# A two-layer graph attention kernel: the destination sums of every superchunk in three pieces, and node merging one step behind

## Chip, cores and metric

The kernel runs on one NeuronCore of a Trainium2 chip. The metric is the device time of one execution in microseconds (us). Five engines work on it with queues of their own: TensorE (PE) for matmuls, VectorE (DVE), ScalarE (ACT), GpSimd (POOL), which issues the row gathers, and SyncE (SP), which issues the other DMAs. Each engine takes its instructions strictly in the order of the program; semaphores make one wait for another.

## The reference

Two graph attention layers over N = 6250 nodes with 256 features and E = 200,000 edges sorted by destination. Cut to what matters (`_gat` gets one self-loop per node whose edge feature is the mean of the node's incoming ones; H is 4 heads of 64 in layer 0 and 1 head of 256 in layer 1):

```python
h = jnp.maximum(_layernorm(x, axis=-1), 0.0)
te = relu(edge_attr @ We + be) * exp(h @ Wo + bo)[src][:, None]
hx = (h @ Wg).reshape(n, H, F)
al = leaky_relu((hx*a_s).sum(-1)[src] + (hx*a_d).sum(-1)[dst]
                + ((te @ Wge).reshape(-1, H, F)*a_e).sum(-1), 0.2)
m  = segment_max(al, dst)
al = exp(al - m[dst]);  al = al / segment_sum(al, dst)[dst]
out = segment_sum(hx[src] * al[:, :, None], dst) + b
```

Layer 0 ends with `relu(out + h)`, layer 1 takes that as its input, and the result is x plus both layers' outputs with their residuals.

## The kernel before

**Tiling.** The 200,000 edges are 1563 chunks of 128. 24 chunks (C = 24) make a superchunk; there are 66 (NS = 66) a layer: 64 of 24 chunks, then one of 14 and one of 13. One step of the main loop in `edges` handles one superchunk, so there are 132 steps, k = 0 to 131, 66 for each layer. In a step, `st` is the superchunk at work, `nx` the next, `pv` the one before and `pf` the one before that. Edges lie so that partition p holds c consecutive edges of the sorted list.

**A prologue** (the first 97 us) normalizes x, multiplies it with the layer's weights and stores a table T0 of node rows in DRAM. Woven into it, `indices` prepares index data on DVE from loads of SP (`sc0`, `bcol`, `drow`, `r4`, `src`, `dpv`); `self.before` is the cast of `dpv`, and `index_group` reads it when it makes `fpen` (L544). Later index groups are made in the loop, seven pieces a step (three of four steps of layer 0).

**What a step does,** with the lines of the profile before:

- `gather(nx)`, L817: POOL issues one indirect DMA a chunk; each brings 128 table rows into `G`. Three `G` buffers rotate, so the gather of step k+1 needs the sums of step k-2 to be done.
- `rphase1(nx)`, L901 and L906: y = edge features times weights on PE in two halves, each followed by a relu on ACT into `R`. There is one `y` buffer. `rphase2` (L915) and `adst` (L974) turn R and the destinations' terms into `zad` on PE; `edge_rows` (L988, L991) transposes it to edges on DVE.
- `logits(st)`, L1002 to L1017: the logits and a forward and a backward segmented max scan on DVE. `ends` (L1025) transposes the scans' ends on PE; `links` (L1035, L1037 on DVE, L1042 on PE) scans over the partitions' borders and transposes the result back; `maxima` (L1052 to L1079) needs it.
- `spread` (L930, L931; once for two steps), `parts` (L955 to L958 on DVE, the matmul L960 on PE) and `blocks` (L967) prepare `nx`.
- `onehots` (L945): the 128 x 128 selection matrices `S` of a superchunk, two buffers.
- `scale` (L1110): the gathered rows times the exponentials; `carried` (L1095 to L1100) adds the share that a node carries over from the superchunk before.
- `sums` (L1120): 24 matmuls `u += S[i]^T G[i]`, which add the edges by destination; the profile counts two passes for each. One PSUM buffer holds `u`. `evict` (L1125) copies it to `U` on ACT; `carry` (L1131, L1133) picks the row that is carried over.
- `finish` (`merge`, `nodes0`, `nodes1`: L1144 to L1237): the self-loop is merged in, the softmax is divided out, the layer's result made, on DVE with small ACT steps. In layer 0, `rows1` (L1215, L1217) and `rows2` (L385) multiply it with layer 1's weights, and `rows3` (`table_row` L389 and L1227, then an SP DMA, L1256) stores the row of table T1. In layer 1, rows1 and rows2 are empty, and rows3 is the store of the output.

**Order.** The program's order is written out by hand (a manual schedule), so the loop body is the queue of every engine. In the loop before, rphase1(nx) comes first, the sums of `pv` stand whole between `parts(nx)` and the transpose in `links(st)`, the one-hots of `st` and finish of `pf` follow on DVE, then maxima, scale, carried, edge_rows(nx). The first step and those with s of 63 and 64 do their sums at once, at the end of the step. `last` handles the last superchunk of a layer (s = 65). In layer 0 it also issues the early gathers of layer 1's first step, whose rows from the last two windows of T1 are zeros that `turned_onehots` and `added` fill in by matmul.

The order of the loop before, as its lines:

```python
self.spread(nx)
self.parts(nx)
if pv and "u" not in pv:
    self.sums(pv)
self.links(st)
...
self.blocks(nx)
if k != self.NS:
    self.onehots(st)
if pf:
    drain(self.finish(pf))
```

Of the kernel before, what the change touches and what calls it, by code (L numbers as in the profile page):

```python
# [22 lines left out]
F32 = mybir.dt.float32  # L23
# [8 lines left out]
P = 128  # L32
C = 24
# [45 lines left out]
class Kernel:  # L79
# [311 lines left out]
    def indices(self, wp):  # L391


        nc, cp, a = self.nc, self.cp, self.a
# [11 lines left out]
        dpv = wp.tile([P, NS], I32, name="dpv", bufs=1)  # L406
        nc.sync.dma_start(dpv, a["dpv"])
        yield
        self.before = cp.tile([P, NS], F32, name="before")
        V.tensor_copy(self.before, dpv)  # L410
        scf = wp.tile([P, 11, NS], F32, name="scf", bufs=1)
        V.tensor_copy(scf, sc0)
        V.memset(scf[:, 0, 0:1], 0.0)
# [72 lines left out]
            V.tensor_scalar(chk[:, 4, :self.direct], base[0:1, :self.direct], float(N - P), None, op0=OP.is_gt)  # L486
        V.memset(self.bad[:, 0:1], 0.0)
        V.tensor_reduce(self.bad[0:1, 0:1], chk.rearrange("p a b -> p (a b)"), axis=AX.X, op=OP.add)
        yield

    def index_tiles(self):
# [79 lines left out]
    def edges(self, ctx):  # L571
        nc = self.nc
        self.gp += [self.pool(f"gath{i}", 1, ctx) for i in range(1, 3)]
        self.sp = self.pool("onehot", 2, ctx)
        self.lp = self.pool("loads", 2, ctx)
        self.wp = self.pool("work", 2, ctx)
        self.np_ = self.pool("nodes", 2, ctx)
        self.xp = self.pool("index", 1, ctx)
        self.ps_y = self.pool("ps_y", 1, ctx, space=PSUM)
        self.ps_1 = self.pool("ps_1", 1, ctx, space=PSUM)  # L580
        self.ps_f = self.pool("ps_f", 1, ctx, space=PSUM)
        self.lf = self.ps_1.tile([P, 512], F32, name="lf")
# [23 lines left out]
        pv = pf = None  # L606
        ahead, rest = 1, None
        for k, st in enumerate(steps):
            nx = steps[k + 1] if k + 1 < len(steps) else None
            for q in steps[k + 1:k + 3]:  # L610
                if q["L"] is st["L"] and "tw" not in q:
                    self.nodes(q)
            self.load_lb(k + 2)
            left = self.groups[ahead][0] - 2 - k if ahead < len(self.groups) else 99
            if rest is None and left <= 2:
                gi = self.index_load(ahead, self.xp)
                rest = self.index_group(ahead, self.xp, gi)
            if st["s"] + 1 == self.NS:
                self.last(st, pv, nx)
                pv = None  # L620
                continue
            self.gather(nx)
            drain(self.rphase1(nx))
            self.load_ea(k + 2)
            drain(self.logits(st))
            self.ends(st)
# [5 lines that stand above are left out]
            self.load_fl(k + 1)  # L632
# [17 lines left out]
            drain(self.scale(st))  # L650
            self.carried(st)
            at_once = k == 0 or self.NS - 3 <= st["s"]
            if at_once:
                self.sums(st)
            if pf:
                self.rows3(pf)
            self.edge_rows(nx)
            if rest is not None:
                for _ in range(7):
                    next(rest, None)  # L660
                if left <= 0:
                    drain(rest)
                    ahead, rest = ahead + 1, None
            pf, pv = pv, st

            if at_once:
                if pf:
                    drain(self.finish(pf))
                    self.rows1(pf)
                    self.rows2(pf)  # L670
                    self.rows3(pf)
                pf = None
                self.evict(st)
                self.carry(st)
            if k == 0 and self.early:
                self.redirect()
        self.flag()

    def last(self, st, pv, nx):

# [2 lines left out]
        if early:  # L683
            self.gather(nx, 0, self.src1)
            v = self.gp[(nx["k"] + 1) % 3].tile([P, C * 270], F32, name="v", tag="G").bitcast(BF)
            nc.sync.dma_start(v[:, :early * P], self.srow.partition_broadcast(P))
        if pv and "U" not in pv:
            self.sums(pv)
            self.evict(pv)
            self.carry(pv)  # L690
        now, half = (C, C) if st["L"].l else (0, C // 2)
        self.onehots(st, 0, now)
        drain(self.logits(st))
        self.ends(st)
        self.onehots(st, now, half)
        self.links(st)
        self.load_fl(st["k"] + 1)
        self.onehots(st, half)
        y = self.rphase1(nx) if nx else iter(())
        next(y, None)  # L700
        next(y, None)
        if nx:
            nc.vector.tensor_scalar(self.src, self.src, 2.0, None, op0=OP.mult)
        drain(self.maxima(st))
        drain(y)
        self.load_ea(st["k"] + 2)
        drain(self.scale(st, 3))
        self.carried(st)
        self.sums(st)
# [3 lines left out]
        if pv:  # L713
            if early:
                w0 = self.turned_onehots(nx, v, 0)
            self.rows1(pv)
            self.rows2(pv)
            self.rows3(pv)
        drain(self.finish(st))
        if early:  # L720
            w1 = self.turned_onehots(nx, v, 1)
# [389 lines left out]
                                    .to_broadcast([P, c1 - c0, H, L.F]), op=OP.mult)  # L1111
            yield

    def sums(self, st):
        nc, L, c = self.nc, st["L"], st["C"]
        G, S = st["G"], st["S"]
        st["u"] = u = self.ps_1.tile([P, 512], F32, name="u")
        for j in range(c):
            i = (j + 1) % c
            nc.tensor.matmul(u[:, :L.W], S[:, i, :], G[:, i, 0:L.W], start=(j == 0), stop=(j == c - 1))  # L1120

    def evict(self, st):
        L = st["L"]
# [263 lines left out]
def drain(g):  # L1387
    for _ in g:
        pass
# [93 lines left out]
```

## Time and profile before

| what | us |
| --- | --- |
| median of 3 runs | 4138.07 (4133.18 to 4142.69) |
| the profiled execution, its time | 4140.48 |
| the profiled execution, span from first to last instruction | 4138.4 |
| first gather of the loop starts | 97.38 |
| first L1035 of layer 0, step 0 | 141.32 |
| L1035 of the last step of layer 0 | 2113.39 |
| last gather starts | 4083.89 |
| mean granted PE clock, as a share of full | 0.78 |

Times in the profile are us from the span's start. A line of the timeline or of the chain of waits gives a start and a duration; in a group, the number after `x` is a count, then come busy us, mean ns of one and the idle time of the engine before them with what ended it. "Issue" is time in which the engine waited for nothing that the profile shows. The groups that this change touches most, besides those shown further on:

```profile
L1120 PE MATMUL u<-G,S 128*128 128x270 f32 (+1 forms) x6252 | 1714.1, 442 | 34.9 <-DVE G L1110 34.9
L901 PE MATMUL y<-ea,webd 64*128 64x384 f32 (+1 forms) x1056 | 512.4, 615 | 457.4 <-ACT R L906 455.3
L1110 DVE TENSOR_TENSOR G<-G,kps 128x6144 f32<-128x6144 f32 (+2 forms) x140 | 853.3, 6100 | 0.0
L988 DVE STREAM_TRANSPOSE rt<-zad 128x768 f32<-128x768 f32 (+1 forms) x130 | 124.4, 957 | 11.6 <-PE zad L974 11.6
```

### The profile page before, as it was taken

What the parts mean: (1) busy time and instruction counts of PE and PEld (TensorE: products, weight loads), DVE (VectorE), ACT (ScalarE), POOL (GpSimd) and SP (SyncE); (2) the same over time, 40 slices, a digit from 0 to 9 for tenths busy, and PEclk for the clock granted to TensorE, in tenths of its full rate; (3) what the DMA queues carried; (4) which work ended last, traced back from release to release, by engine and by line L of the source; (5) the groups of instructions that cost most, each with busy time, mean ns of one, the idle gap of its engine ahead of it and who ended that gap; (6) DMA issues with size and microseconds to landing.
All of it is one profiled execution on the core that took longest, in us unless ns stands there. A gap on an engine that the chain in (4) does not pass through costs nothing.

```text
span 4138.4 us, 34955 instructions
## 1 busy us (share of the span) xinstructions
PE 2815.1 (68%) x10144; PEld 1863.5 (45%) x10144; DVE 2872.6 (69%) x6572; ACT 545.2 (13%) x1256; POOL 2988.4 (72%) x3158
## 2 busy tenths in 40 slices
PE   7577777777676776777676666656566666756665
PEld 5344444444454444544454444434344444434344
DVE  7587777777877778778766666666666666666665
ACT  5111111111111111111111010100101010010100
POOL 2777777777777777777647777777777777777773
PEclk9677877778787787777877777878777777777777
DMA  6545555555554555555435455445545554554552
GB/s 203 155 135 153 149 142 147 147 146 143 154 149 137 154 147 141 149 149 149 125 102 151 132 143 141 137 137 144 141 133 141 141 137 137 145 141 133 141 139 61
DMA packets 246794, 584.74 MB, mean 141 GB/s; under 512 B 63161, under 2 KB 103639, under 8 KB 246529
## 3 DMA queue, kind: packets, MB, share of 16 engines
q0 software_dynamic: 150144, 422.82, 38.7%
q1 hardware_dynamic: 96035, 158.96, 12.3%
q8 instruction: 81, 1.33, 0.1%
q14 instruction: 118, 0.97, 0.1%
q10 hardware_dynamic: 416, 0.67, 0.1%
HBM read 547.98 MB, written 34.34 MB: 141 GB/s over the span
## 4 chain that ended last, share of the span: by engine, by line
POOL 35%; PE 27%; DVE 19%; issue 14%; DMA 2%; ACT 2%; DVEq 0%; ACTq 0%; SPq 0%; POOLq 0%
POOL G L817 35%; PE u L1120 21%; DVE G L1110 9%; PE y L901 3%; DVE lb L930 1%; DMA G<-T,src 1%; PE fin L1131 1%; DVE rt L988 1%; ACT R L906 1%; PE fin L1215 1%; DVE G L1099 1%; ACT carry L1133 1%; DVE G L1079 0%; DVE t1row L389 0%; DVE crow L1095 0%
## 5 line engine op out<-in xcount | busy, mean ns | idle before, releaser
L817 POOL DMA_INDIRECT G<-T,src x3114 | 2970.0, 954 | 1092.2 <-issue 996.5
L1120 PE MATMUL u<-G,S 128*128 128x270 f32 (+1 forms) x6252 | 1714.1, 442 | 34.9 <-DVE G L1110 34.9
L1120 PEld LDWEIGHTS u<-G,S 128*128 128x128 f32 x6252 | 1370.1, 222 | 386.8 <-issue 41.1
L1110 DVE TENSOR_TENSOR G<-G,kps 128x6144 f32<-128x6144 f32 (+2 forms) x140 | 853.3, 6100 | 0.0
L901 PE MATMUL y<-ea,webd 64*128 64x384 f32 (+1 forms) x1056 | 512.4, 615 | 457.4 <-ACT R L906 455.3
L901 PEld LDWEIGHTS y<-ea,webd 64*128 64x128 f32 x1056 | 214.3, 224 | 677.8 <-ACT R L906 535.7
L945 DVE TENSOR_TENSOR S<-kps,loc 128x3072 f32<-128x3072 f32 (+2 forms) x133 | 436.4, 3281 | 0.0
L1025 PE MATMUL lf<-ident,fb 128*36 128x128 f32 (+1 forms) x132 | 54.0, 409 | 533.8 <-DVE fb L1017 306.3
L1025 PEld LDWEIGHTS lf<-ident,fb 128*36 128x36 f32 (+1 forms) x132 | 15.8, 119 | 651.6 <-DVE fb L1017 363.3
L906 ACT ACTIVATE R<-y,webd 128x768 f32<-128x768 f32 x260 | 231.9, 892 | 566.4 <-PE y L901 566.2
L1056 DVE SCALAR_TENSOR_TENSOR m<-fpen,lf,m 128x24 f32<-128x24 bf16 (+1 forms) x66 | 16.5, 250 | 378.9 <-PE lf L1042 378.6
L1002 DVE TENSOR_TENSOR G<-rt,G 128x96 f32<-128x96 f32 (+1 forms) x132 | 30.2, 229 | 262.8 <-DMA G<-T,src 256.7
L915 PE MATMUL zad<-R,wea 128*64 128x384 f32 (+1 forms) x1056 | 205.4, 510 | 0.3 <-DVE aq L967 0.3
L1059 DVE TENSOR_TENSOR mt<-fpen,lf 128x96 f32<-128x96 bf16 (+1 forms) x66 | 16.7, 253 | 253.8 <-PE lf L1042 253.8
L1125 ACT ACTIVATE U<-u 128x270 f32<-128x270 f32 (+1 forms) x132 | 51.8, 392 | 815.8 <-PE u L1120 815.8
L960 PE MATMUL zad<-a,Q 128*128 128x12 bf16 (+1 forms) x132 | 23.7, 179 | 169.3 <-DVE a L958 169.3
L1158 ACT ACTIVATE mw<-mw,mg 128x2 f32<-128x2 f32 x66 | 19.7, 298 | 885.7 <-DVE mg L1157 885.7
L988 DVE STREAM_TRANSPOSE rt<-zad 128x768 f32<-128x768 f32 (+1 forms) x130 | 124.4, 957 | 11.6 <-PE zad L974 11.6
L930 DVE TENSOR_TENSOR lb<-lb,kps 128x1536 bf16<-128x1536 bf16 (+1 forms) x68 | 113.0, 1662 | 12.8 <-DMA lb<-locrow 12.8
L915 PEld LDWEIGHTS zad<-R,wea 128*64 128x64 f32 x1056 | 66.2, 139 | 92.5 <-issue 58.8
L1131 PE MATMUL fin<-U,lsel 128*1 128x270 f32 (+1 forms) x260 | 79.1, 385 | 41.5 <-ACT U L1125 22.5
L1035 DVE TENSOR_TENSOR_SCAN cl<-fl,cl,lf 4x129 f32<-4x129 f32 (+1 forms) x130 | 60.7, 467 | 56.3 <-PE zad L960 52.9
(213 smaller groups left out, 2269.9 us busy)
## 6 DMA issues: line engine op xcount, KB each, us to landing
G<-T,src POOLq DMA_INDIRECT x3114, 2.8
ea<-in_ea_dram SPq DMA_DIRECT2D x64, 768.0 KB
lb<-locrow SPq DMA_DIRECT2D x64, 384.0 KB
T<-t1row SPq DMA_DIRECT2D x66, 260.0 KB
tw<-T SPq DMA_DIRECT2D x66, 258.0 KB
tw<-T SPq DMA_DIRECT2D x66, 134.0 KB
tw<-in_x_dram SPq DMA_DIRECT2D x66, 128.0 KB
out_dram<-fb SPq DMA_DIRECT2D x64, 128.0 KB
```

What stands on the lines that cost most here:

```text
L817: nc.gpsimd.indirect_dma_start(out=G[:, c, 0:L.TW], out_offset=None, in_=self.rows[L.l][0:n * (1 + L.l), :], in_offset=bass.IndirectOffset ...
L901: nc.tensor.matmul(y[:, o], self.webd[l][r, :], ea[r, w], start=True, stop=True)
L906: nc.scalar.activation(R[:, i, :32 * c].rearrange("p (b n) -> p b n", b=2), y.rearrange("p (b n) -> p b n", b=2)[:, :, :16 * c], AF.Relu, ...
L915: nc.tensor.matmul(st["zad"][i * PH:(i + 1) * PH, o], self.wea[l][0], R[:, i, w], start=True, stop=False)
L930: V.tensor_tensor(lb[:, :, :n], lb[:, :, :n], self.k_part.unsqueeze(2).to_broadcast([P, i, n]), op=OP.is_equal)
L945: nc.vector.tensor_tensor(st["S"][:, c0:c1, :], self.k_iota.unsqueeze(1).to_broadcast(w), self.loc[:, o + c0:o + c1].unsqueeze(2).to_broad ...
L988: V.transpose(rv[:, :32 * c].rearrange("p (b n) -> p b n", b=2), z.rearrange("p (b n) -> p b n", b=2)[:, :, :16 * c])
L1025: self.nc.tensor.transpose(self.lf[0:e.shape[1], 1:P + 1], e, self.ident)
L1035: V.tensor_tensor_scan(cl[:H, :], fl[:H, :], lf[:H, 0:P + 1], init, op0=OP.add, op1=OP.max)
L1110: nc.vector.tensor_tensor(v, v, pw[:, c0:c1, :].unsqueeze(3) .to_broadcast([P, c1 - c0, H, L.F]), op=OP.mult)
L1120: nc.tensor.matmul(u[:, :L.W], S[:, i, :], G[:, i, 0:L.W], start=(j == 0), stop=(j == c - 1))
L1131: nc.tensor.matmul(pr[0:1, :L.W], self.lsel[:, s:s + 1], U[:, :L.W], start=True, stop=True)
```

## The change

All steps but the first and the last of each layer take a new body, `tight`. The sums of a superchunk come in three pieces (`pieces` gives 12 and 16 for 24 chunks): chunks 0 to 11 at the end of its own step, 12 to 15 in the next step between `parts(nx)` and the transpose of `links`, 16 to 23 behind that transpose. The one-hots are made for `nx` at the end of the step, and `finish` works on `pv` (one step behind, not two), also at the end of the step. rphase1(nx) moves from the head of the step to behind rows2. `last` takes the same pieces through `meet`. In the prologue, the cast of `dpv` moves from the start of `indices` to its end.

```diff
@@ indices
-        self.before = cp.tile([P, NS], F32, name="before")
-        V.tensor_copy(self.before, dpv)
...
+        yield
+        self.before = cp.tile([P, NS], F32, name="before")
+        V.tensor_copy(self.before, dpv)
@@ edges, the loop
+        tight = 1
...
             if st["s"] + 1 == self.NS:
                 self.last(st, pv, nx)
-                pv = None
+                pv = pf = pr = None
+                continue
+            if st["s"] >= tight:
+                self.tight(st, pv, pr, nx)
+                self.index_on(left)
+                pr, pv = pv, st
                 continue
...
-            at_once = k == 0 or self.NS - 3 <= st["s"]
-            if at_once:
+            enter = st["s"] + 1 == tight
+            if enter:
+                self.sums(st, 0, self.pieces(st)[0])
...
+            if enter:
+                self.onehots(nx)
...
+    def pieces(self, st):
+        c = st["C"]
+        return (c + 1) // 2, c - c // 3
+
+    def meet(self, st, pv, nx):
+        p1, p2 = self.pieces(pv) if pv else (0, 0)
+        drain(self.logits(st))
+        self.ends(st)
+        if nx:
+            self.spread(nx)
+            self.parts(nx)
+        if pv:
+            self.sums(pv, p1, p2)
+        self.links(st)
+        if pv:
+            self.sums(pv, p2)
+        self.load_fl(st["k"] + 1)
+
+    def tight(self, st, pv, pr, nx):
+        final = nx["s"] + 1 == self.NS
+        self.gather(nx)
+        self.meet(st, pv, nx)
+        self.blocks(nx)
+        if final:
+            self.evict(pv)
+            self.carry(pv)
+            if pr:
+                self.rows1(pr)
+                self.rows2(pr)
+                self.rows3(pr)
+            drain(self.finish(pv))
+            drain(self.maxima(st))
+            self.rows1(pv)
+            self.rows2(pv)
+        else:
+            drain(self.maxima(st))
+            self.evict(pv)
+            self.carry(pv)
+            if pr:
+                self.rows1(pr)
+                self.rows2(pr)
+        drain(self.rphase1(nx))
+        self.load_ea(st["k"] + 2)
+        self.rphase2(nx)
+        self.adst(nx)
+        if final:
+            self.rows3(pv)
+        drain(self.scale(st))
+        self.carried(st)
+        self.sums(st, 0, self.pieces(st)[0])
+        if pr and not final:
+            self.rows3(pr)
+        self.edge_rows(nx)
+        self.onehots(nx)
+        if not final:
+            drain(self.finish(pv))
@@ last
-        if pv and "U" not in pv:
-            self.sums(pv)
-            self.evict(pv)
-            self.carry(pv)
...
-        self.onehots(st, half)
-        y = self.rphase1(nx) if nx else iter(())
-        next(y, None)
-        next(y, None)
+        if not pv:
+            self.onehots(st)
+        self.meet(st, pv, None)
...
         drain(self.maxima(st))
-        drain(y)
-        self.load_ea(st["k"] + 2)
+        if pv:
+            self.evict(pv)
+            self.carry(pv)
         drain(self.scale(st, 3))
...
             self.rows3(pv)
+        if nx:
+            drain(self.rphase1(nx))
+            self.load_ea(st["k"] + 2)
         drain(self.finish(st))
@@ sums
-    def sums(self, st):
+    def sums(self, st, a=0, b=C):
...
-        for j in range(c):
+        for j in range(a, min(b, c)):
             i = (j + 1) % c
-            nc.tensor.matmul(u[:, :L.W], S[:, i, :], G[:, i, 0:L.W], start=(j == 0), stop=(j == c - 1))
+            nc.tensor.matmul(st["u"][:, :L.W], S[:, i, :], G[:, i, 0:L.W], start=(j == 0), stop=(j == c - 1))
```

More of the change, by code (lines that the diff above doesn't have):

```diff
@@ L604, in edges @@
         self.edge_rows(steps[0])
-        pv = pf = None
-        ahead, rest = 1, None
+        pv = pf = pr = None
+        tight = 1
+        self.ahead, self.rest = 1, None
         for k, st in enumerate(steps):
@@ L613, in edges @@
             self.load_lb(k + 2)
[L614 to L617, printed above, removed]
+            left = self.groups[self.ahead][0] - 2 - k if self.ahead < len(self.groups) else 99
+            if self.rest is None and left <= 2:
+                gi = self.index_load(self.ahead, self.xp)
+                self.rest = self.index_group(self.ahead, self.xp, gi)
             if st["s"] + 1 == self.NS:
                 self.last(st, pv, nx)
-                pv = None
+                pv = pf = pr = None
+                continue
[3 more added lines that the diff above has]
+                pr, pv = pv, st
                 continue
@@ L651, in edges @@
             self.carried(st)
-            at_once = k == 0 or self.NS - 3 <= st["s"]
-            if at_once:
+            enter = st["s"] + 1 == tight
+            if enter:
+                self.sums(st, 0, self.pieces(st)[0])
+            elif st["s"] == 0:
                 self.sums(st)
@@ L657, in edges @@
             self.edge_rows(nx)
[L658 to L672, printed above, removed]
+            if enter:
+                self.onehots(nx)
+                if pv:
+                    drain(self.finish(pv))
+                pr = pv
+            elif st["s"] == 0:
                 self.evict(st)
                 self.carry(st)
+            self.index_on(left)
+            pf, pv = pv, st
             if k == 0 and self.early:
@@ L677, in edges, with index_on @@
         self.flag()
+    def index_on(self, left):
+        if self.rest is not None:
+            for _ in range(7):
+                next(self.rest, None)
+            if left <= 0:
+                drain(self.rest)
+                self.ahead, self.rest = self.ahead + 1, None
+    def pieces(self, st):
[51 more added lines that the diff above has]
+        if not final:
+            drain(self.finish(pv))
     def last(self, st, pv, nx):
@@ L686, in last @@
             nc.sync.dma_start(v[:, :early * P], self.srow.partition_broadcast(P))
-        if pv and "U" not in pv:
-            self.sums(pv)
-            self.evict(pv)
-            self.carry(pv)
[L691 to L697, printed above, removed]
-        self.onehots(st, half)
-        y = self.rphase1(nx) if nx else iter(())
-        next(y, None)
-        next(y, None)
+        if not pv:
+            self.onehots(st)
+        self.meet(st, pv, None)
         if nx:
@@ L704, in last @@
         drain(self.maxima(st))
-        drain(y)
-        self.load_ea(st["k"] + 2)
+        if pv:
+            self.evict(pv)
+            self.carry(pv)
         drain(self.scale(st, 3))
@@ L1112, in scale @@
             yield
-    def sums(self, st):
+    def sums(self, st, a=0, b=C):
         nc, L, c = self.nc, st["L"], st["C"]
         G, S = st["G"], st["S"]
-        st["u"] = u = self.ps_1.tile([P, 512], F32, name="u")
-        for j in range(c):
+        if a == 0:
+            st["u"] = self.ps_1.tile([P, 512], F32, name="u")
+        for j in range(a, min(b, c)):
             i = (j + 1) % c
-            nc.tensor.matmul(u[:, :L.W], S[:, i, :], G[:, i, 0:L.W], start=(j == 0), stop=(j == c - 1))
+            nc.tensor.matmul(st["u"][:, :L.W], S[:, i, :], G[:, i, 0:L.W], start=(j == 0), stop=(j == c - 1))
     def evict(self, st):
```

## The prediction

> **What bounds the kernel now.** I read the page first. No engine is full: GpSimd (POOL) leads with 72%, almost all of it row gathers, and the idle time in front of the gathers is "issue", time that waits for nothing.
>
> ```profile
> PE 2815.1 (68%) x10144; PEld 1863.5 (45%) x10144; DVE 2872.6 (69%) x6572; ACT 545.2 (13%) x1256; POOL 2988.4 (72%) x3158
> L817 POOL DMA_INDIRECT G<-T,src x3114 | 2970.0, 954 | 1092.2 <-issue 996.5
> ```
>
> Then I read the chain of waits by layer. In layer 1 it is gathers alone, each with its issue gap:
>
> ```profile
> 2999.75 0.95 POOL G L817
> 3000.70 0.30 issue
> ```
>
> One gather is issued every 1.25 us, so a step of 24 cannot be shorter than 30.04 us. In layer 0 the chain leaves POOL and runs PE, VectorE (DVE), PE. One step of it:
>
> ```profile
> 1018.05 0.17 PE zad L960
> 1018.22 12.45 PE u L1120 x48
> 1030.66 0.19 PE lf L1042
> ...
> 1033.66 6.40 DVE G L1110
> ...
> 1041.44 0.90 DVE rt L988
> ...
> 1048.00 0.01 PE zad L960
> ```
>
> The 24 sums (48 passes) stand between the matmul of parts (L960) and the transpose of links (L1042) that maxima waits for. The starts of L1035 give 30.35 us a step from step 2 to step 63 of layer 0 (194.75 to 2045.90, 61 steps), 0.3 over POOL's pace. The waits of that stretch show what is at stake:
>
> ```profile
> DVE mt L1059 <- PE lf L1042: 249.0, 61, 5.2
> POOL G L817 <- PE lf L1042: 22.9, 23, 5.4
> ```
>
> DVE waits 4.1 us a step for that transpose, but POOL loses only about 23 us in the whole layer. That is the most layer 0 can win, since past it the gathers bound; layer 1 can win nothing in steady state.
>
> **What hides what today.** While PE runs the sums, DVE runs the one-hots (3.26 us from start to next start) and finish (4.94 us, 1022.21 to 1027.15), then waits. PE in turn has the next step's y (L901) done early: two matmul pairs per step, one in this step's slack, one behind a long idle.
>
> ```profile
> 1018.95 3.35 DVE L945 TENSOR_TENSOR S<-kps,loc 128x3072 f32<-128x3072 f32 x1
> 1004.20 1.55 PE L901 MATMUL y<-ea,webd 64*128 64x384 f32 x4
> 1011.29 2.92 PE L901 MATMUL y<-ea,webd 64*128 64x384 f32 x4 [5.54 <-ACT R L906]
> ```
>
> **The new step in layer 0, from one L960 to the next.** Only 4 of 24 sums stay before the transpose, 8 follow it, and 12 move to the end of the step before. But PE's program order is now: 4 sums, transpose, 8 sums, lsel, rows1, rows2, y, y, rphase2, adst, first 12 sums of the step. DVE's edge_rows (L988 before) waits for adst, and behind it in DVE's queue stand onehots(nx), finish(pv), the index pieces and the next step's logits; for those PE waits (ends, parts), and POOL waits for the sums that free a buffer. So I add PE's chain up to adst, and the DVE work behind it:
>
> - 24 passes on the path. I took the 60 whole layer-0 groups of 48 passes row by row: the first 24 last 7.87 us (6.71 to 8.74), the last 24 5.47, since PE starts them at half clock after idling. In the new step PE idles before them as well (the first 12 sums end some 8 us before the next L960), so 7.87. Transpose 0.19.
> - From the end of the sums to the end of rows2, with rows of 1030.7 to 1033.2 and 1003.2: eviction with its gaps 0.48, lsel 0.63, carry with gaps 0.46, rows1 0.45, h1T with gaps 0.52, rows2 1.04: 3.58.
> - y 1.55, relu with gaps 1.05, y 1.55, relu 1.05 (layer 1 shows this pair, 3016.14 to 3021.24): 5.20.
> - rphase2: one of its four matmuls needs only the first half of R and runs under the second relu; three take 1.06 of 1.44; adst 0.50: 1.56.
>
> That is 18.40 us until edge_rows may start. DVE itself is there after 3.83 (8 passes) + 0.19 + 10.6 (L1042's end to L988: 1030.85 to 1041.44) = 14.65, so it stalls 3.75. Then edge_rows 1.44, one-hots 3.26, finish 4.94, logits 1.90 with 0.3 of semaphore gaps, spread 1.98 in every second step (0.99), parts and L960 0.92, index pieces (1.9, 0.9 and 0.45 in three of four steps) 0.8: 14.55. Together 32.95. The one-hots and finish, 8.20 us, were free under the sums; now they lie on the path, and for that 5.47 us of sums left it. Against 30.35: +2.6 us a step, 61 steps, +159 us.
>
> **The clock in that chain.** The prices above are at full clock. These two stretches of PE's windows show it drop:
>
> ```profile
> 1003.87:1007.28 3.41, 1.88 (x6) 0.67 (x4) 3.41 (x1) 0.00 (x0) 2.50 (x4) 1.00 0.39 107
> 1007.28:1010.70 3.42, 0.00 (x0) 0.00 (x0) 3.39 (x7) 0.46 (x2) 2.67 (x3) 0.50 0.44 120
> ```
>
> The columns are length, busy PE, PE loads, DVE, ACT, POOL, then the granted clock. A stretch of 3.41 us in which PE was busy 1.88 (55%) is followed by clock 0.50; one with 1.55 (46%, 3017.73 to 3021.14) too; one with 2.33 (68%, 1034.58 to 1038.00) keeps 1.00. Between the sums and the first 12 sums PE would be busy 0.63+0.45+1.04+3.10+1.56 = 6.8 of 10.3 us, 66%, just at that line. Ends of the term: nothing, if the clock holds; if it falls at once, 1.37 for each y (2.92 against 1.55), 1.0 and 0.3 for rphase2 and adst (2.83 and 0.82 at 142.47 and 145.23 against 1.51 and 0.50, three quarters of the first), and an estimate of 2.1 for lsel, rows1 and rows2 at double their rows: 6.1. I take 2.0: the second y, rphase2 and adst slow (2.7) in three steps of four, because the gaps (1.05 twice) lie there. 61 steps: +122 us.
>
> [...]
>
> **The rest.**
> - Prologue: the cast of dpv moves behind the checks. Now DVE stands 7.41 us for its DMA (33.7 to 41.1), and DVE is on the chain from there to 88 us. The next instruction reads sc0, queued first of that batch; its landing isn't seen, so 0 to -7.4. I take -6.5, as no other wait on a load stands in the rows after it. Nothing reads `before` until L544 at 96 us.
> - Steps 0 to 2: the one-hots and finish fall on the path while nothing of sums(0) was in step 1's way before (it ran at once, under step 0's end). With the rows at 154 to 194 step 2 starts 3 us later (0 to +5).
> - End of layer 0: sums(63) need not run whole behind scale(63) (2069.51, 14.22 us) and rows(63) move up. From L960 of step 63 to the first gather of layer 1 now: 2046.2 to 2113.6, 67.4. New: to adst 15.4 (14 chunks), edge_rows to the next L960 13.6, in step 64 7.87+3.58 to rows2(62), t1row 0.4, finish(63) 4.9, rows 2.1, y and relu 4.2, t1row's exp, store and landing 3: 55. The rest of the transition gives some back to the half clock: -10 (-4 to -14).
> - Tail: from logits(129) at 4052.95 to the end now 85.4. New: 22.1 for step 129 (2.8 to L960, 7.65, 0.19+0.48+0.60, y and relu 3.6, 1.1, edge_rows 0.9, one-hots 1.9, finish 2.95), 22.1 for step 130 (finish now ahead of maxima and waiting for all sums), and 19.7 for the last (logits to the first scaled piece 6.4, 26 passes 8.55, eviction, finish, store 4.8): 63.9. With half clock for the y's, -18 (-12 to -22).
> - Layer 1, steady: no rows, finish 2.95. The same sum is 7.65+0.19+1.1+5.2+1.56, edge_rows 1.2, 3.26, 2.95, logits 1.4, spread 0.99, parts 0.9: 26.4, and 4 more with a low clock; below 30.04. So 0, hidden by POOL.
> - SP: the ea load waits for the later y, with the t1row store behind it, but it has a step's time until it is read: 0. Moving index pieces and load_fl: 0.
>
> Sum on the profiled span: 4138.4 + 159 + 122 - 6.5 + 3 - 10 - 18 = 4388 us. The profiled execution took 4140.5 with its 2 us around the span, the median of the runs 4138.07, so the span stands for the median. I forecast **4385**.
>
> **Rivals.**
> - *The chain is on the path, the clock holds* (0.2): 4388 - 122 = 4266. For it: 66% is at the edge, the longest gap is 1.05. Against: two drops at 46 and 55%.
> - *The whole chain runs at half clock* (0.13): 6.1 x 61 = 372 in place of 122: 4638 at the end; with half of the excess, 4510. For it: once low, PE rose only after a full stretch (0.50 still at 2.88 of 3.41, 1017.52 to 1020.93).
> - *DVE does not stall and POOL bounds layer 0* (0.1): 61 steps at 30.04 save 19: 4138 - 19 - 6.5 - 13 - 21 = 4079, faster. It decides when the loop is under 30.04, 2.9 us less than my sum; if PE were warm, the 24 passes would take 5.47, 2.4 less. For it: DVE's wait of 4.1 goes. Against: PE idles before them in every step of the trace.
> - *It nets to nothing* (0.02): the warm loop at about 30.8 with the gains at both ends.
>
> The forecast has 0.55. **Range** 4210 to 4540: below lies the faster case and a part of the warm one, above the half-clock end. A change under 0.2% (8 us) is what a measurement of this kernel cannot tell from none. Faster 0.1, same 0.02, slower 0.88.
>
> **What would show it.** Layer 0's L1035 rows 33 to 36 us apart; DVE's L988 row (L1052 after) waiting for adst 3.5 us or more in each layer-0 step; the wait of L1059 down to about 2; y rows of 2 to 2.9 us; POOL waiting several us a step for sums in layer 0 and none in layer 1, whose steps stay at 30.04; a first gather near 91 us; some 15 us less from the last gather to the end. Wrong if edge_rows doesn't wait, or if layer-0 steps are at 30.

## The result, and the profile after

The changed kernel takes 4400.64 us (median of 4 runs, 4395.32 to 4404.33); the kernel before, on the same chip, 4140.38 us (4133.18 to 4143.16). The ratio is 1.064, with a 95% interval of 1.0621 to 1.0659: 6.4% slower. The forecast was 4385. The profiled execution took 4403.65 us, its span is 4401.8.

From the page, the busy line and three groups, the last beside its line in the kernel before (in a group: count, busy us, mean ns of one, and after the second bar the idle time before them with what ended it):

```profile
PE 3128.6 (71%) x10144; PEld 1901.9 (43%) x10144; DVE 2879.3 (65%) x6571; ACT 559.1 (13%) x1256; POOL 2973.3 (68%) x3158
L881 POOL DMA_INDIRECT G<-T,src x3114 | 2955.0, 949 | 1383.1 <-issue 966.0
L1052 DVE STREAM_TRANSPOSE rt<-zad 128x768 f32<-128x768 f32 (+1 forms) x130 | 127.1, 978 | 779.3 <-PE zad L1038 779.3
L979 PE MATMUL zad<-R,wea 128*64 128x384 f32 (+1 forms) x1056 | 434.6, 737 | 7.7 <-ACT R L970 7.4
L915 PE MATMUL zad<-R,wea 128*64 128x384 f32 (+1 forms) x1056 | 205.4, 510 | 0.3 <-DVE aq L967 0.3
```

The work is the same, the count of matmuls too, yet PE is busy 313 us longer (2815.1 before). Of these, some 229 us are rphase2's (L979, L915 before), whose recorded time now also takes in part of the second relu. The clock isn't lower on the whole (mean granted clock 0.799, 0.780 before); what changed is where in the step it is low. POOL's gathers stand idle 291 us longer (1092.2 before), and their issue gaps are no part of that. One DVE instruction, the first of edge_rows, has 779 us of waiting in front of it.

Where the 263.4 us of the span (4401.8 - 4138.4) are, from the starts of DVE's first links scan (L1035 before, L1099 after) and of the gathers:

| stretch | before | after | difference | predicted |
|---|---|---|---|---|
| to the first gather | 97.38 | 88.58 | -8.8 | -6.5 |
| from there to the scan of step 0 | 43.94 | 42.64 | -1.3 | not priced |
| steps 0 to 2 of layer 0 | 53.4 | 59.1 | +5.7 | +3 |
| steps 2 to 63 (61 steps) | 30.35 each | 35.11 each | +290.5 | +281 |
| step 63 to the first gather of step 67 | 107.6 | 103.6 | -4.0 | -10 |
| from there to the last gather | 1930.4 | 1925.8 | -4.6 | 0 |
| last gather to the end | 54.5 | 40.4 | -14.1 | -18 |

So the time is lost in the middle steps of layer 0. The list of waits of the changed kernel, 200 to 2050 us, DVE and POOL (who waited for what: us in total, times, longest):

```profile
DVE rt L1052 <- PE zad L1038: 352.7, 53, 10.0
DVE mt L1123 <- PE lf L1106: 154.7, 52, 3.1
...
POOL G L881 <- PE u L1185: 276.4, 52, 10.2
```

Before, the first was absent, the second (as L1059) was 4.1 us a step and the third 23 us in all. Now DVE stands 6.7 us a step for adst and POOL 5.3 us a step for the sums that free a gather buffer. PE's timeline of one such step, start and length:

```profile
1035.68 4.76 PE L1185 MATMUL u<-G,S 128*128 128x270 f32 x16
1040.93 0.62 PE L1196 MATMUL fin<-U,lsel 128*1 128x270 f32 x2 [0.49 <-ACT U L1190]
1042.02 0.44 PE L1280 MATMUL fin<-ident,fb 128*128 128x128 f32 x2 [0.48 <-ACT carry L1198]
1042.99 1.14 PE L385 MATMUL fin<-wg,h1T 128*128 128x260 f32 x4 [0.53 <-ACT h1T L1282]
1044.06 1.55 PE L965 MATMUL y<-ea,webd 64*128 64x384 f32 x4
1046.67 1.97 PE L965 MATMUL y<-ea,webd 64*128 64x384 f32 x4 [1.05 <-ACT R L970]
1048.56 3.27 PE L979 MATMUL zad<-R,wea 128*64 128x384 f32 x8
1051.77 0.50 PE L1038 MATMUL zad<-lb,aq 128*128 128x384 bf16 x2
```

And DVE's, which starts edge_rows when the last of these ends, then does the one-hots, then finish, and reaches the next logits at 1062.95:

```profile
1052.30 0.98 DVE L1052 STREAM_TRANSPOSE rt<-zad 128x768 f32<-128x768 f32 x1 [6.43 <-PE zad L1038]
...
1053.69 3.35 DVE L1009 TENSOR_TENSOR S<-kps,loc 128x3072 f32<-128x3072 f32 x1
...
1062.95 0.26 DVE L1066 TENSOR_TENSOR G<-rt,G 128x96 f32<-128x96 f32 x1
```

The second y takes 1.97 us where the first takes 1.55. The row of rphase2, 3.27 us, is not to be held against its 1.51 in the kernel before, since its first matmul now starts while the second relu still runs:

```profile
1048.67 0.90 ACT L970 ACTIVATE R<-y,webd 128x768 f32<-128x768 f32 x1 [2.06 <-PE y L965]
```

From the end of that relu to the end of rphase2 it is 2.27 us here. Over the 61 steps it is 1.56 in the 20 steps with the clock at 1.00 there, and 2.55 in the 41 with a mean of 0.50 to 0.74. Two windows of PE show the clock fall (length, busy PE, loads, DVE, ACT, POOL, granted clock):

```profile
1044.27:1047.68 3.41, 2.36 (x7) 1.13 (x7) 1.57 (x6) 0.90 (x1) 2.61 (x3) 1.00 0.40 102
1047.68:1051.09 3.41, 3.41 (x9) 1.16 (x8) 0.00 (x0) 0.99 (x2) 2.50 (x4) 0.50 0.47 121
```

PE was busy 69% of the first; the next has half the clock although PE is recorded as busy all through it.

### The profile page after: what moved, and what is told of

It reads as the page before. It is cut to its first block, busy times and chain, and to the rows that moved or that the text cites. A ratio compares the mean times of both kernels' runs of the same rounds, so it can differ in the third digit from the quotient of the medians.

```text
span 4401.8 us, 35044 instructions
## 1 busy us (share of the span) xinstructions
PE 3128.6 (71%) x10144; PEld 1901.9 (43%) x10144; DVE 2879.3 (65%) x6571; ACT 559.1 (13%) x1256; POOL 2973.3 (68%) x3158
## 4 chain that ended last, share of the span: by engine, by line
POOL 31%; PE 30%; DVE 17%; issue 13%; DMA 5%; ACT 4%; DVEq 0%; ACTq 0%; SPq 0%; POOLq 0%
POOL G L881 31%; PE u L1185 16%; PE y L965 5%; DMA G<-T,src 5%; PE zad L979 4%; DVE S L1009 3%; DVE lb L994 2%; ACT R L970 2%; PE fin L385 1%; DVE rt L1052 1%; PE fin L1196 1%; PE zad L1038 1%; DVE fb L1079 1%; DVE al L1070 1%; DVE al L1068 1%
## 5 line engine op out<-in xcount | busy, mean ns | idle before, releaser
L1185 PE MATMUL u<-G,S 128*128 128x270 f32 (+1 forms) x6252 | 1757.2, 440 | 16.0 <-DVE G L1174 16.0
L1185 PEld LDWEIGHTS u<-G,S 128*128 128x128 f32 x6252 | 1335.2, 219 | 294.3 <-DVE G L1174 17.9
L965 PE MATMUL y<-ea,webd 64*128 64x384 f32 (+1 forms) x1056 | 534.5, 638 | 141.1 <-ACT R L970 136.3
L979 PE MATMUL zad<-R,wea 128*64 128x384 f32 (+1 forms) x1056 | 434.6, 737 | 7.7 <-ACT R L970 7.4
L1009 DVE TENSOR_TENSOR S<-kps,loc 128x3072 f32<-128x3072 f32 x132 | 436.3, 3305 | 0.0
L979 PEld LDWEIGHTS zad<-R,wea 128*64 128x64 f32 x1056 | 140.6, 189 | 289.5 <-issue 174.9
L1139 ACT ACTIVATE kps<-mt 128x100 f32<-128x100 f32 (+1 forms) x132 | 29.8, 226 | 1419.1 <-DVE mt L1133 725.1
L1123 DVE TENSOR_TENSOR mt<-fpen,lf 128x96 f32<-128x96 bf16 (+1 forms) x66 | 16.6, 252 | 188.2 <-PE lf L1106 188.2
L385 PE MATMUL fin<-wg,h1T 128*128 128x260 f32 x264 | 88.1, 464 | 36.7 <-ACT h1T L1282 36.7
L1024 PEld LDWEIGHTS <-Q 128*128 128x128 bf16 x132 | 13.6, 103 | 215.4 <-DVE a L1022 198.5
```

The costliest lines, as they stand in the source:

```text
L385: self.nc.tensor.matmul(ps[:, :L.MW], hT[:, k, :], self.wg[L.l][:, k, :], start=(k == 0), stop=(k == 1))
L965: nc.tensor.matmul(y[:, o], self.webd[l][r, :], ea[r, w], start=True, stop=True)
L979: nc.tensor.matmul(st["zad"][i * PH:(i + 1) * PH, o], self.wea[l][0], R[:, i, w], start=True, stop=False)
L1009: nc.vector.tensor_tensor(st["S"][:, c0:c1, :], self.k_iota.unsqueeze(1).to_broadcast(w), self.loc[:, o + c0:o + c1].unsqueeze(2).to_broad ...
L1185: nc.tensor.matmul(st["u"][:, :L.W], S[:, i, :], G[:, i, 0:L.W], start=(j == 0), stop=(j == c - 1))
```

## The experiments

Each kernel ran beside the kernel before on the same chip, where that took 4138 to 4143 us (experiment 10 apart); ratios are to it. "A step" is the mean from step 2 to step 63 of layer 0.

**1. y back at the head of the step.**

```diff
 def tight
         self.gather(nx)
+        drain(self.rphase1(nx))
+        self.load_ea(st["k"] + 2)
         self.meet(st, pv, nx)
...
-        drain(self.rphase1(nx))
-        self.load_ea(st["k"] + 2)
         self.rphase2(nx)
```

> The changed kernel with one thing put back: in the middle steps the next step's rphase1 (both y matmuls and both relus) and its ea load stand at the head of the step again, ahead of logits, as before the change. Theory A (the loss is PE's chain sums, evict, rows, y, relu, y, relu, rphase2, adst, which keeps DVE from edge_rows with the one-hots and finish queued behind): without y the chain is 5.2 us shorter and more of it runs at full clock, the wait of the transpose in edge_rows (L1052) falls from 6.7 us to under 1.5 us a step, layer-0 steps fall from 35.1 to the gathers' pace, 30.0 to 30.6, and the time is 4085 to 4130 us, below the kernel before. Rival B (the loss is that the 8.2 us of one-hots and finish no longer lie beside the 24 sums, whatever stands before them): the steps stay above 33.5 us and the time above 4300. Rival C (splitting the sums in three costs it: PE cold at each piece): also above 4300, with the PE rows of the sums unchanged and the wait of L1123 still 3 us.

4078.91 us, ratio 0.985 (0.9834 to 0.9867), 6 us under the expected range; 30.01 us a step, as expected. Waits, 200 to 2050 us:

```profile
DVE mt L1123 <- PE lf L1106: 177.0, 61, 3.1
...
DVE rt L1052 <- PE zad L1038: 20.9, 24, 1.3
...
POOL G L881 <- issue: 440.8, 1447, 0.3
```

The wait for adst falls from 6.7 to 0.3 us a step, and POOL waits for nothing but its own issue. From the first sum behind parts to the end of adst it takes 14.2 us on average, 20.85 in the changed kernel. The pieces of the sums stand as they were, with their 2.9 us wait of L1123: neither they (rival C) nor the place of the one-hots and finish (rival B) costs anything that shows at the pace of the gathers, once y is out of the chain.

**2. One-hots and finish ahead of edge_rows.** y stays late.

```diff
-        self.edge_rows(nx)
         self.onehots(nx)
         if not final:
             drain(self.finish(pv))
+        self.edge_rows(nx)
```

> The changed kernel with one order turned on DVE: onehots of the next step and finish of the step before are issued ahead of edge_rows instead of behind it; PE's order stays. Theory A (DVE stands 6.7 us a step for adst with 8.2 us of work queued behind that needs none of it): the one-hots and finish fill the wait, the layer-0 step loses 5 us or more and is held by the gathers at 30.0 to 30.6 us, the time is 4085 to 4130 us. Rival B (PE's chain is the bound by itself, from one adst to the next, and DVE only waits on it): steps stay at 34 us or more, the time at 4350 or more. Rival D (the index pieces or the rows chain set the step): no change either.

4080.09 us, ratio 0.985 (0.9834 to 0.9866), 5 us under the expected range; 30.07 us a step. Waits of DVE and POOL:

```profile
DVE G L1066 <- DMA G<-T,src: 113.5, 54, 6.4
...
DVE rt L1052 <- PE zad L1038: 0.9, 5, 0.2
...
POOL G L881 <- issue: 429.2, 1408, 0.3
```

PE's chain is nearly as long as before the edit (20.2 us to adst, 20.85 before), and it costs nothing: the wait is filled by 8.2 us of work that never needed adst. DVE now waits for gathered rows instead. So the chain was not the bound by itself (rival B of this run); its product with the order on DVE was.

**3. Only the one-hots ahead of edge_rows**, finish behind it.

```diff
-        self.edge_rows(nx)
         self.onehots(nx)
+        self.edge_rows(nx)
         if not final:
             drain(self.finish(pv))
```

> The changed kernel with only the one-hots of the next step (3.26 us) ahead of edge_rows, and finish behind it as it was. Theory A (what DVE does ahead of edge_rows instead of behind it leaves the path, microsecond for microsecond, until the wait of 6.7 is used up): L1052's wait falls by 3.3 to about 3.4 us, steps from 35.1 to 31.8, the time to 4195 to 4215 us. Rival (only the order as a whole matters, or PE's half clock takes back what is won): 4250 us or more.

4170.98 us, ratio 1.0063 (1.0046 to 1.0081); 31.36 us a step.

```profile
DVE rt L1052 <- PE zad L1038: 184.3, 59, 6.8
...
POOL G L881 <- PE u L1185: 77.6, 52, 3.0
```

The wait falls by 3.5 to 3.1 us a step, about the one-hots' own length, but the step falls by 3.75, which is more than expected; the time is 24 us under the expected range. The rest may be the clock, which was not tried: its mean is 0.817 over this run and 0.799 in the changed kernel, and PE's chain to adst is 20.4 us, 0.4 shorter. Between the changed kernel and experiment 2 the reordered work pays roughly microsecond for microsecond, until the gathers bound.

**4. Busy matmuls in the gaps of the chain.** `warm(n)` issues n matmuls of 128 columns whose result nothing reads, in layer 0 only.

```diff
+    def warm(self, st, n):
+        if st["L"].l == 0:
+            for _ in range(n):
+                self.nc.tensor.matmul(self.lf[:, 256:384], self.ident, self.ident, start=True, stop=True)
...
             self.evict(pv)
+            self.warm(st, 2)
             self.carry(pv)
+            self.warm(st, 2)
             if pr:
                 self.rows1(pr)
+                self.warm(st, 2)
                 self.rows2(pr)
-        drain(self.rphase1(nx))
+        for _ in self.rphase1(nx):
+            self.warm(st, 4)
```

> The changed kernel with matmuls added whose result nothing reads, in layer 0's middle steps only: two each after the eviction of u, after lsel and after the transposes of rows1, four after each of the two y matmuls, so that PE is busy in the gaps of its chain. If the half clock in the chain is what the partly idle windows bring (the term of 2.0 us a step): the clock stays at 1.00 from the sums to adst, the second y takes 1.5 instead of 2.0 us, rphase2 1.6 instead of 3.2, layer-0 steps fall by 1.5 to 2.5 us and the time to 4250 to 4310 us. Rival: the clock falls for another reason (its drops come at a fixed time after the sums start, or the windows still hold the idle time before the sums): the second y and rphase2 keep their lengths, the added matmuls lengthen the chain by 0 to 1 us a step and the time is 4400 to 4460.

4292.15 us, ratio 1.0362 (1.0345 to 1.0379); 33.27 us a step, 1.84 less than the changed kernel. PE's timeline of one step (L698 is the added work):

```profile
1036.08 1.55 PE L974 MATMUL y<-ea,webd 64*128 64x384 f32 x4
1037.56 1.16 PE L698 MATMUL lf<-ident 128*128 128x128 f32 x8
1038.68 1.55 PE L974 MATMUL y<-ea,webd 64*128 64x384 f32 x4
1040.17 1.16 PE L698 MATMUL lf<-ident 128*128 128x128 f32 x8
1041.26 1.51 PE L988 MATMUL zad<-R,wea 128*64 128x384 f32 x8
1042.70 0.50 PE L1047 MATMUL zad<-lb,aq 128*128 128x384 bf16 x2
```

And two of PE's windows there, columns as above:

```profile
1035.79:1039.20 3.41, 3.41 (x16) 2.02 (x15) 2.53 (x6) 0.90 (x1) 2.50 (x4) 1.00 0.37 109
1039.20:1042.61 3.41, 3.41 (x20) 1.74 (x18) 0.00 (x0) 0.99 (x2) 2.64 (x3) 1.00 0.51 134
```

With more work on PE the kernel is 2.6% faster than the changed one, by the two ratios. The second y is back at 1.55 us in every step, and from the end of the second relu to the end of rphase2 it is 1.59 us, as in the full-clock steps of the changed kernel (1.56). The chain to adst takes 19.05 us on average against 20.85, so holding the clock won 1.8 us a step, net of what the added matmuls cost. The first 8 passes keep their 3.9 us: nothing fills the idle time ahead of them.

**5. Busy matmuls ahead of the sums too**: experiment 4 and one line more.

```diff
         self.sums(st, 0, self.pieces(st)[0])
+        self.warm(st, 22)
```

> The changed kernel with the matmuls in the chain's gaps as in the run before, and 22 more behind the first 12 sums of each layer-0 step, so that PE is also busy for most of the 6 us ahead of the next ends. Theory (the clock is at half when the second 12 sums start because PE idled before them, as the term of 7.87 us for 24 passes from cold says, against 5.47 warm): the first 8 passes take 2 instead of 3.95 us, the wait of L1123's successor falls from 3.1 to under 2 us, the step from 33.3 to 31 to 31.5 us, the time to 4150 to 4190 us. Rival (the start of the sums is slow for another reason, such as their operands): the 8 passes keep 3.9 us and the time stays within 15 us of 4292, or above it.

4233.98 us, ratio 1.0227 (1.0202 to 1.0252); 32.39 us a step. That is between the two: 58 us better than experiment 4, where 100 to 140 were expected. Two groups of the first 8 passes:

```profile
1028.60 3.76 PE L1195 MATMUL u<-G,S 128*128 128x270 f32 x8
...
1094.91 2.07 PE L1195 MATMUL u<-G,S 128*128 128x270 f32 x8
```

The 22 matmuls last 5.1 us, and the idle time that they should fill is 6 to 11. Of the 61 steps, 16 did the 8 passes in under 2.6 us, and the 24 passes and the transpose in 6.09 on average; 36 took over 3.6 us for the 8 (3.95 in the changed kernel where the clock is 0.50 all through them) and 8.0 in all. So a slow start costs 1.9 us a step, where the prediction's sum had 2.4 (7.87 against 5.47); the filling was too short to win it in every step.

**6. The sums in one piece again**, with y at the head as in experiment 1: 23 of 24 sums lie between ends and links.

```diff
 def pieces
-        return (c + 1) // 2, c - c // 3
+        return 1, c
```

> The changed kernel with y at the head of the step, and with the sums nearly whole again: 1 of 24 at the end of the step before, 23 between ends and links, none behind. Theory A (the split is what pays for the one-hots and finish, which no longer lie under the sums): 23 sums from cold 12.6 us, transpose 0.2, DVE's maxima to edge_rows 10.6, then 14.5 of edge_rows, one-hots, finish, logits, spread and parts on the path: 37 to 39 us a layer-0 step, the time 4480 to 4700 us. Rival C (the split does nothing; y's place alone makes the difference): as with the three pieces, 30 to 31 us a step and 4070 to 4140 us.

4697.12 us, ratio 1.1345 (1.131 to 1.1381); 37.57 us a step, inside the expected 37 to 39. DVE waits 11.6 us a step for the transpose of links (569.4 in 49 steps). The split in three is worth 7.6 us a step against experiment 1: it is what pays for taking the one-hots and finish out from under the sums.

**7. The kernel before with y late, and nothing else.** First with y ahead of maxima in program order:

```diff
 edges, the loop
         self.gather(nx)
-        drain(self.rphase1(nx))
-        self.load_ea(k + 2)
         drain(self.logits(st))
...
             if pf:
                 self.rows1(pf)
+            drain(self.rphase1(nx))
+            self.load_ea(k + 2)
             self.rphase2(nx)
             self.adst(nx)
             drain(self.maxima(st))
```

> The kernel before with one part of the change alone: rphase1 of the next step and its ea load moved from the head of the step to behind the sums, the eviction and rows1, straight ahead of rphase2 (24 sums whole, one-hots and finish where they were). Theory A (the price of the later y is only what of PE's chain sticks out beside DVE's maxima, scale and carried): after the transpose of links PE needs about 2.0 for the eviction to rows1, 5.2 for the two y and relus and 1.6 for rphase2 and adst, 8.8 us at full clock, against 10.6 us of DVE, so little of it shows: layer-0 steps 30.3 to 32, the time 4130 to 4240 us. Rival B (y behind the sums costs its 5.2 us and the half clock wherever the one-hots and finish stand): 35 us or more a step, 4420 us or more.

4522.2 us, ratio 1.0918 (1.0891 to 1.0946); 35.8 us a step. The figure is rival B's, but the wait is another one than either theory named. DVE's longest wait, 200 to 2050 us:

```profile
DVE G L1079 <- ACT kps L1075: 319.4, 52, 6.5
```

ACT's timeline of one step:

```profile
1032.74 0.90 ACT L906 ACTIVATE R<-y,webd 128x768 f32<-128x768 f32 x1 [1.10 <-PE y L901]
1036.37 0.90 ACT L906 ACTIVATE R<-y,webd 128x768 f32<-128x768 f32 x1 [2.72 <-PE y L901]
1037.17 0.25 ACT L1075 ACTIVATE kps<-mt 128x100 f32<-128x100 f32 x1
```

The Exp of maxima (L1075), whose input was ready at 1031, stands behind the two relus in ACT's order, and DVE's copy of its result stands 6.1 us a step for it. The expectation had counted PE and DVE and forgotten ACT.

**8. The same with y behind maxima**, so that ACT takes the Exp first. The lines at the head of the loop go as in experiment 7; below, rphase2 and adst move too:

```diff
             if pf:
                 self.rows1(pf)
-            self.rphase2(nx)
-            self.adst(nx)
             drain(self.maxima(st))
+            drain(self.rphase1(nx))
+            self.load_ea(k + 2)
+            self.rphase2(nx)
+            self.adst(nx)
```

> The kernel before with y moved behind the sums again, but now behind the DVE pieces of maxima as well, so that ACT takes the Exp of maxima ahead of the two relus; the rows2 matmuls come behind adst as before. In the last run of this kind the copy behind the Exp (L1079) waited 6.2 us a step, because the relus stood ahead of it in ACT's queue. If that order was the whole of its cost: L1079's wait is gone, PE's 8.8 us from the sums' end to adst (at half clock from the second y on some 11) lie beside DVE's 10.6, steps of 30.3 to 32 us and 4130 to 4240 us. Rival B (the later y costs 5 us a step wherever it stands behind the sums): edge_rows (L988) waits instead, 35 us a step, 4420 us or more.

4246.66 us, ratio 1.0251 (1.0222 to 1.028); 32.38 us a step. Waits of DVE:

```profile
DVE mt L1059 <- PE lf L1042: 248.4, 57, 5.1
DVE t1row L389 <- PE fin L385: 129.5, 57, 2.6
DVE G L1079 <- ACT kps L1075: 33.0, 58, 0.9
```

The wait for the Exp is gone, and with it 3.4 of the 5.45 us that experiment 7 had cost. The other 2.0 us a step are what sticks out of PE's chain: rows2 comes last in it, and rows3's first instruction (L389), which stands ahead of edge_rows, waits 2.3 us a step for it. The time is 7 us above the expected range. So a late y costs 2 us a step in the old order, where DVE has 10.6 us of its own work beside it.

**9. rows1 and rows2 behind adst** in the changed kernel.

```diff
             self.carry(pv)
-            if pr:
-                self.rows1(pr)
-                self.rows2(pr)
...
         self.adst(nx)
+        if pr and not final:
+            self.rows1(pr)
+            self.rows2(pr)
```

> The changed kernel with rows1 and rows2 (two transposes, the copy h1T, two matmuls of 260 columns) behind adst instead of ahead of y. By the sum they are 0.45 + 0.52 + 1.04 = 2.0 us of the chain: layer-0 steps of 33.1 us and 4270 to 4290 us if the clock does as before. Rival: PE is idle more in the chain without them and the clock falls a window earlier, which gives 1 us or more back: 4320 us or more. Rival D (rows bound the step through the table row's store): no change, 4390 to 4410.

4390.04 us, ratio 1.0594 (1.0563 to 1.0626); 34.85 us a step. The step is not at 33.1, and the time, though it lies where the rivals had it, has the reason of none of them: adst ends 18.4 us after the first sum, 2.5 earlier, and the wait has moved one instruction up. DVE's longest wait:

```profile
DVE t1row L389 <- PE fin L385: 333.3, 53, 7.8
```

Two rows of DVE's timeline:

```profile
1040.30 0.43 DVE L389 TENSOR_TENSOR t1row<-fin,bias 128x260 f32<-128x260 f32 x1 [4.19 <-PE fin L385]
1040.64 0.97 DVE L1052 STREAM_TRANSPOSE rt<-zad 128x768 f32<-128x768 f32 x1
```

rows3 is issued ahead of edge_rows, and now waits for rows2, which ends after adst. Moving the matmuls without their reader only changed which instruction of DVE waits.

**10. With the reader moved as well**: rows3 behind edge_rows and the one-hots.

```diff
-        if pr and not final:
-            self.rows3(pr)
         self.edge_rows(nx)
         self.onehots(nx)
+        if pr and not final:
+            self.rows3(pr)
         if not final:
             drain(self.finish(pv))
```

> The changed kernel with rows1 and rows2 behind adst, as in the run before, and now also with rows3 (whose first DVE instruction, L389, reads what rows2 wrote) behind edge_rows and the one-hots, so that edge_rows no longer queues behind it. In the run before adst ended 18.4 us after the first sum instead of 20.9, but L389 stood 6.3 us a step for rows2 ahead of edge_rows. Theory A (rows1, h1T and rows2 are 2.0 to 2.5 us of the chain, and L389's place gave them back): edge_rows waits for adst again, 4 to 4.7 us, the layer-0 step falls from 35.1 to 32.5 to 33.2 us and the time to 4240 to 4285 us. Rival (the step is held by the clock's idle windows, which close the gap): 34.5 us or more, 4360 us or more.

Inconclusive. It took 5708.72 us, on a chip on which the kernel before took 4911.98 instead of some 4140 (ratio 1.1622, 1.1603 to 1.1641). There DVE's instructions start late with nothing that they wait for, as in this row of its timeline, and a ratio taken there says nothing of the order tested:

```profile
1076.08 0.32 DVE L1068 TENSOR_TENSOR al<-G 128x96 f32<-128x96 f32 x1 [2.17 <-issue]
```

PE's stretch from the first sum to adst is 18.2 us there, as in experiment 9. What that is worth in time stays open.

**11. The cast alone**, in the kernel before.

```diff
 indices
-        self.before = cp.tile([P, NS], F32, name="before")
-        V.tensor_copy(self.before, dpv)
         scf = wp.tile([P, 11, NS], F32, name="scf", bufs=1)
...
         V.tensor_reduce(self.bad[0:1, 0:1], chk.rearrange("p a b -> p (a b)"), axis=AX.X, op=OP.add)
         yield
+        self.before = cp.tile([P, NS], F32, name="before")
+        V.tensor_copy(self.before, dpv)
+        yield
```

> The kernel before with the cast of dpv alone moved behind the checks. If the cast's 7.4 us wait for its DMA was on the path to the first gather: the first gather starts at 88 to 91 us instead of 97.4 and the time falls by 6 to 10 us (ratio 0.9976 to 0.9986). Rival: the next load of the batch lands just as late, so the wait only moves to the next instruction: first gather within 1 us of before and the time within 2 us.

4135.55 us, ratio 0.9985 with an interval of 0.997 to 1.0001, which just takes in no change; the profile is clearer. The first gather starts at 88.84 us (97.38 before). The cast of scf, which the old order held until 41.23, is here, in DVE's timeline:

```profile
33.16 0.52 DVE L410 CAST scf<-sc 128x726 f32<-128x726 int32 x1
```

So sc0 had landed by then, and the wait does not reappear at the next load. At the links scan of step 63 the gain is still 10.5 us, at the last gather 5.8, at the end of the span 6.3: layer 1, paced by the gathers, gave some back, and why was not tried.

**12. Experiments 1 and 2 together**, both diffs in one kernel.

> Both orders turned in the changed kernel: y at the head of the step, and one-hots and finish ahead of edge_rows. Each alone gave 4079 to 4080 us. Theory A (each alone takes the loop below the gathers' pace, which then sets it): the two together give no more, layer-0 steps 30.0 to 30.2 us, the time 4072 to 4086 us, with no waits of POOL but its own issue. Rival: each alone was held by what the other takes away; together the steps fall below 29.5 us and the time below 4050 us.

4072.76 us, ratio 0.9839 (0.9815 to 0.9863); 29.92 us a step. POOL's waits:

```profile
POOL G L881 <- issue: 441.3, 1449, 0.3
```

The 29.92 us a step are a little under the 30.04 that the prediction called the least a step can take. Each edit alone had already reached the gathers' pace, and the two together gain nothing that the intervals tell apart. It is the fastest kernel of the study: 1.6% under the kernel before and, by the two ratios (0.9839 / 1.064), 7.5% under the changed one.

## Why the prediction was right, point by point

**The sum of the layer-0 step** gave 20.4 us to adst (18.40 and 2.0 for the clock) and 14.55 behind it: 34.95. Measured: 20.85 and 14.26, together 35.11. The 24 passes with their transpose took 8.18 us (8.06 in the sum), the rest of the chain 12.67 (12.34 with the clock term). One term of the rest was too small: the last three matmuls of rphase2 were to take 1.06 us behind the second relu, but at full clock they take 1.44 (275.78 to 277.21 in the changed kernel, to the start of adst). Experiments 1 and 2 show that both halves are needed: without y in the chain, or with the 8.2 us of DVE's work out from behind edge_rows, the whole loss goes.

**DVE's stall** was put at 5.75 us and is 6.7. The 14.65 us that DVE was given to reach edge_rows are 14.2 (20.85 - 6.7), and adst comes 0.45 later than summed.

**The clock term**, 2.0 us a step chosen between 0 and 6.1, is 1.8 by experiment 4, net of what the added matmuls cost. The clock was to be low in three steps of four, and rphase2 behind the second relu met clock 0.50 in 41 of 61, in 21 of them all through. Without the term the forecast would have been 122 us lower. In the changed kernel's chain PE waits at most 1.3 us at a time (ahead of the second y, 200 to 2050 us), and the clock fell after a window that was 69% busy; with the gaps filled it stayed at 1.00 in the step shown of experiment 4. So here it fell without a long gap.

Nor does the share of busy time decide, by which the prediction judged the chain to be "just at that line". Three windows in a row of the changed kernel (columns as above):

```profile
405.98:409.39 3.41, 2.02 (x8) 0.96 (x8) 3.41 (x1) 1.09 (x3) 2.63 (x3) 1.00 0.23 62
409.39:412.80 3.41, 2.36 (x7) 1.15 (x7) 2.25 (x6) 0.90 (x1) 2.50 (x4) 1.00 0.38 103
412.80:416.22 3.42, 3.42 (x8) 1.28 (x8) 0.00 (x0) 0.99 (x2) 2.50 (x4) 0.50 0.57 120
```

The clock held after a window that was 59% busy and fell after the next, which was 69% busy. So the size of the term was a good choice, but in part luck. The second window is mostly y, whose lines read `64*128` where those of the sums read `128*128`. Of the changed kernel's 328 windows at full clock between 150 and 2050 us, the best single limit on busy time puts 35 on the wrong side; with the time of each matmul multiplied by the first of these two figures over 128, 13. No run changed that figure alone: the added matmuls are `128*128` and also fill the gaps, so what sets the clock is not shown. That it rose only after a full stretch, as the half-clock rival had it, nearly holds: in the kernel before, from 150 to 4100 us, it rose 134 times, after windows that were 84 to 100% busy, the stretch of 2.88 us of 3.41 among them.

**The wait of L1123** was to fall to about 2 us and is 3.0. The 8 passes ahead of the transpose take 3.84 us on average, as the sum had them (3.83), so it is DVE's work beside them that is shorter than the sign assumed, about 1 us. The wait lies inside the 20.85 and adds nothing to it.

**The prologue** was put at -6.5 of a possible -7.4, and the first gather came 8.8 us earlier (8.5 with the cast alone, experiment 11). That is over the bound, which was the wait's own length. But one trace says little here: on the chips with some 4140 us for the kernel before, the traces with the cast moved start their first gather between 88.58 us (the changed kernel) and 90.81 (experiment 1), 6.6 to 8.8 us earlier than the 97.38.

**Steps 0 to 2, the transition and the tail** had the right signs and were each some 3 to 6 us too good: +5.7 for +3, -4.0 for -10, -14.1 for -18. These chains were added up from single rows at full clock, and their dependence on the clock was only guessed. Which of their terms is short was not measured.

**Layer 1** was said to hide its longer chain under POOL. DVE does wait there, 340 us for adst between 2470 and 4300 us, 5.6 a step (6.7 in layer 0), but POOL waits for the sums there only 5.8 us in all, and the step stays at 30.05 us, since finish and the rest are shorter. So the same wait that costs 5 us a step in one layer costs nothing in the other.

**Of the rivals**, the one on the other side (DVE does not stall, POOL bounds layer 0, 4079 us) is the state that experiments 1, 2 and 12 reached with one order turned, or both: 4079, 4080 and 4073. It was given the right price, and the point from which it decides (a loop under 30.04 us) was the right one.

## What to carry to other kernels

Before a producer chain is moved later, look at what is queued behind its reader on the reader's engine: work that doesn't need the result belongs ahead of the waiting instruction, and then a chain of 20 us costs nothing. Count every engine that the moved step passes, ACT too: an Exp behind two relus cost 3.4 us a step here, and a reader left at its old place took the wait over one for one. And price a serial PE chain with its clock: in the changed kernel, whose chain has a gap of 1.05 us ahead of the second y, rphase2 behind the second relu took 2.55 us where it met clock 0.50 and 1.56 at 1.00, and with the gaps filled the step was 1.8 us shorter.

## What was not expected of the hardware

Matmuls with no use made the kernel faster: 1776 more matmul instructions in layer 0 took 4400.6 us to 4292.2, since the granted clock, in the step shown, stayed at 1.00 through a chain in which it had fallen to 0.50. And one chip was slower throughout: in experiment 10 the kernel before took 18.6% longer than elsewhere (4912 us against 4140), and only the run of the kernel before beside it tells that.
